# Attention vectors broadcast by DMA, six lead tiles, an early table load and a split last store in a graph-attention and expert-FFN kernel

## The chip, the cores and the metric

The kernel runs on one core of one Trainium2 chip. The metric is device time in microseconds of one execution. A profiled execution gives a trace: its span runs from the first to the last instruction.

## The reference, cut to what matters

```python
# x [30000, 256]; src, dst, edge_type_8 [510000], sorted by dst; 8 relations, 4 heads, head size 64
def _L0_gnn_ref(inputs, conv_weights, attn_l, attn_r, h_bias, edge_src, edge_dst, edge_type):
    feat_all = jnp.einsum('ni,rhid->rnhd', inputs, conv_weights)
    feat_src_e = feat_all[edge_type, edge_src]
    feat_dst_e = feat_all[edge_type, edge_dst]
    el = jnp.sum(feat_src_e * attn_l[edge_type], axis=-1)
    er = jnp.sum(feat_dst_e * attn_r[edge_type], axis=-1)
    e = jax.nn.leaky_relu(el + er, negative_slope=LEAKY_SLOPE)
    ...            # softmax of e over the edges of one destination node gives alpha
    h = jax.ops.segment_sum(alpha[..., None] * feat_src_e, edge_dst, num_segments=N_NODES)
    return h.reshape(N_NODES, OUT_FEAT) + h_bias

x = x + _L0_gnn_ref(_layernorm(x), ...)
x = x + _L0_ffn_ref(_layernorm(x)[None], ...)[0]     # a shared MLP and the best two of four experts
```

For every node, relation and head a vector of 64 features is computed, with two numbers beside it: its product with `attn_l` (the source's share of an edge's score) and with `attn_r` (the destination's share).

## The kernel before

There are two stages, one after the other. A third part of the code is skipped on these inputs: its loops run `again` times, which is zero here.

The **feature stage** goes over the nodes in 235 tiles of 128 (the last has 48 new rows). Each tile is normalised (`norm`: statistics, reciprocal and scaling on VectorE, DVE; the square root on ScalarE, ACT), turned on TensorE, PE, into `xT` (`turn`), and multiplied by all weights in `NG` = 5 groups of columns (`group`, L299: four of 7 heads x 64 = 448 columns, the last of 4 x 64 and 64 more). A float32 matmul goes through PE in two passes, and a group has two matmuls, one for each half of the 256 inputs: four passes. Groups are evicted from PSUM (pool `pf`, six buffers) into `fo`, by ACT or DVE (L301). The 64 columns at the end of `w` give the two attention numbers: L303 puts the source's into `fo`, L307 the destination's into `er`. SyncE's queue, SP, stores `fo` to `feat` in DRAM, 1040 KB a tile (L309). Once for four tiles `dest_pieces` splits `er` into three bfloat16 parts in five DVE operations (L322, L324) and SP stores them to `erp_d`. After the second tile of each four, `residual` lets GpSimd, POOL, add the bias `hb` (L268), and SP stores the sum (`xb_d`) and loads the next four tiles of `x` (`xg`), in that order.

The 64 columns must first be computed: they are the weights' products with `attn_l` and `attn_r`. `attention(s)` does this in 16 slots. Each even slot spreads 512 numbers of an attention vector over all partitions with a matmul of a column of ones (one row deep) by `arow` (L333); two slots use it: a product (L335) and a sum (L337) on DVE. So that PE has work meanwhile, the first `LEAD` = 5 tiles do only their groups 0 to 3, a slot behind each group from slot 0 on; when all slots are done, the lead tiles' group 4 follows for all of them, and from tile 5 on a tile is done whole.

The **edge stage** goes over the edges in 253 blocks. For each, POOL gathers 16 sets of 128 rows of `feat` by index (L751, 4050 gathers in all), DVE computes scores and softmax, PE sums by destination, and the expert MLPs of finished nodes are woven in. Its pools lie where the feature stage's did, so the first gather waits for that stage's last stores, evictions and matmuls. SP loads a block's `rc`, `dr`, `erp` and `xt` two blocks ahead.

In both stages `tc.manual_schedule()` keeps every engine's instructions in the order of the program. DMAs of SP and ACT take eight completion semaphores in turn: a DMA waits until the eighth before it has landed. The stage's first DMAs are issued so: SP the first four tiles of `x`, then the four chunks of `w` for the first half of the inputs, with `attn_l` after the first; ACT the chunks of the second half and `attn_r`. ACT's first `activation` is the square root in `norm(0)` (L129), and the load of its table stands right before it.

Of the kernel before, what the change touches and what calls it, by code (L numbers as in the profile page):

```python
# [10 lines left out]
F32 = mybir.dt.float32  # L11
# [3 lines left out]
AF = mybir.ActivationFunctionType  # L15
# [6 lines left out]
P = 128  # L22
# [3 lines left out]
HD = 64  # L26
HW = HD + 1
# [13 lines left out]
T = 4  # L41
# [7 lines left out]
def kernel(  # L49
# [26 lines left out]
    nc = tc.nc  # L76
    N = x.shape[0]
    E = src.shape[0]
    NT = -(-N // P)
# [25 lines left out]
    eps = const.tile([P, 1], F32, name="eps")  # L105
# [11 lines left out]
    def bcast(dst_ap, src_ap, n):  # L117

        nc.sync.dma_start(dst_ap, bass.AP(tensor=src_ap.tensor, offset=src_ap.offset, ap=[[0, P], [1, n]]))
# [47 lines left out]
    for i in range(NPEN + 1):  # L167
        f = wf.tile([P, H, U if i < NPEN else UL], F32, name=f"penf{i}")
# [44 lines left out]
    with ExitStack() as cx:  # L213
        wp = cx.enter_context(tc.tile_pool(name="wconv", bufs=1))
        xp = cx.enter_context(tc.tile_pool(name="xa", bufs=2))
# [3 lines left out]
        pf = cx.enter_context(tc.tile_pool(name="pf", bufs=6, space=PSUM))  # L219
        RH = R * H  # L220
        NW = RH * HD
        GH = 7
        NG = -(-RH // GH)
        LEAD = 5

        w = wp.tile([P, 2, NW + 2 * RH], F32, name="w")
        arow = wp.tile([1, 2, NW], F32, name="arow")
        ones = wp.tile([1, P], F32, name="ones")
        nc.vector.memset(ones, 1.0)
        featv = feat.rearrange("(n r) f -> n (r f)", r=R)  # L230
        tiles = {}
        quad = {}

        def start(m):
            return min(m * P, N - P)

        def fresh(m):

            return m * P - start(m)

        def per_rows(q, dram_of, sb_of, store):

            if (q + 1) * T * P <= N:
                d, s = dram_of(q * T * P, T * P).rearrange("(j p) f -> p j f", p=P), sb_of(slice(0, P), slice(0, T))
                nc.sync.dma_start(*((d, s) if store else (s, d)))
                return
            for j in range(min(T, NT - q * T)):
                m = q * T + j
                f = fresh(m) if store else 0
                d, s = dram_of(start(m) + f, P - f), sb_of(slice(f, P), j)  # L250
                nc.sync.dma_start(*((d, s) if store else (s, d)))

        def load_x(q):
            if q * T >= NT:
                return
            xg = quad[q] = xp.tile([P, T, D], F32, name="xg")
            if q == 0:
                for j in range(T):
                    nc.sync.dma_start(xg[:, j], x[j * P:(j + 1) * P, :])
            else:  # L260
                per_rows(q, lambda r, n: x[r:r + n, :], lambda p, j: xg[p, j], False)
# [18 lines left out]
        def turn(m, eng):  # L280
# [4 lines left out]
            for k in range(2):  # L285
                nc.tensor.transpose(ptr[:, k, :], t["xn"][:, 0, k * P:(k + 1) * P], ident)  # L286
            t["xT"] = xp.tile([P, 2, P], F32, name="xT", bufs=LEAD + 1)
            eng(t["xT"], ptr)  # L288

        def group(m, g, eng):  # L290

            t = tiles[m]
            if g == 0:
                t["fo"] = xp.tile([P, RH, HW], F32, name="fo", bufs=LEAD + 1)
            h0, h1 = g * GH, min((g + 1) * GH, RH)
            c0, c1 = h0 * HD, h1 * HD if g < NG - 1 else NW + 2 * RH
            ps = pf.tile([P, 512], F32, name="ps")[:, :c1 - c0]
            for k in range(2):
                nc.tensor.matmul(ps, t["xT"][:, k, :], w[:, k, c0:c1], start=k == 0, stop=k == 1)  # L299
            n = (h1 - h0) * HD  # L300
            eng(t["fo"][:, h0:h1, :HD], ps[:, :n].rearrange("p (a d) -> p a d", d=HD))  # L301
            if g == NG - 1:
                nc.vector.tensor_copy(t["fo"][:, :, HD], ps[:, n:n + RH])  # L303
                q, j = divmod(m, T)
                if j == 0:
                    quad[q, "er"] = xp.tile([P, T, RH], F32, name="er")
                nc.vector.tensor_copy(quad[q, "er"][:, j, :], ps[:, n + RH:])  # L307
                f = fresh(m)
                nc.sync.dma_start(featv[start(m) + f:start(m) + P, :],  # L309
                                  t["fo"][f:].rearrange("p a d -> p (a d)"))  # L310
                del tiles[m]
                if j == T - 1 or m == NT - 1:
                    dest_pieces(q, j + 1)

        def dest_pieces(q, n):

            er = quad.pop((q, "er"))
            del quad[q]
            erp = xp.tile([P, T, H, 3, R], BF16, name="erp")
            erv = er.rearrange("p j (r h) -> p j h r", h=H)[:, :n]  # L320
            for k in range(3):
                nc.vector.tensor_copy(erp[:, :n, :, k, :], erv)  # L322
                if k < 2:
                    nc.vector.tensor_sub(erv, erv, erp[:, :n, :, k, :])  # L324
            per_rows(q, lambda r, n: erp_d[r:r + n].rearrange("n h k r -> n (h k r)"),
                     lambda p, j: erp.rearrange("p j h k r -> p j (h k r)")[p, j], True)

        def attention(s):

            i, q, k = s // 8, s // 2 % 4, s % 2  # L330
            if k == 0:
                quad["ab"] = pf.tile([P, 512], F32, name="ps")
                nc.tensor.matmul(quad["ab"], ones, arow[:, i, q * 512:(q + 1) * 512], start=True, stop=True)  # L333
            pr = xp.tile([P, 8, HD], F32, name="pr")
            nc.vector.tensor_mul(pr, quad["ab"].rearrange("p (a d) -> p a d", d=HD),  # L335
                                 w[:, k, q * 512:(q + 1) * 512].rearrange("p (a d) -> p a d", d=HD))
            nc.vector.tensor_reduce(w[:, k, NW + i * RH + q * 8:NW + i * RH + q * 8 + 8], pr, AX.X, ALU.add)  # L337

# [136 lines left out]
            nc.vector.tensor_reduce(bad, two, AX.X, ALU.max)  # L475

        with tc.manual_schedule():
            load_x(0)
            for k in range(2):
                eng = nc.scalar if k else nc.sync  # L480
                for g in range(4):
                    eng.dma_start(w[:, k, g * 512:(g + 1) * 512].rearrange("p (a d) -> p a d", d=HD),
                                  conv_w[2 * g:2 * g + 2, :, k * P:(k + 1) * P, :].rearrange("r h p d -> p (r h) d"))
                    if g == 0:
                        a = attn_r if k else attn_l
                        eng.dma_start(arow[:, k, :], a.rearrange("(o r) h d -> o (r h d)", o=1))
            bcast(hb, h_bias, D)
            norm(0)
            turn(0, nc.scalar.copy)
            norm(1)  # L490

            slot = 0
            lead = min(LEAD, NT)
            for m in range(lead):
                for g in range(NG - 1):
                    group(m, g, nc.scalar.copy)
                    if slot < 16:
                        attention(slot)
                    slot += 1
                    if g == 1 and m + 1 < lead:  # L500
                        turn(m + 1, nc.scalar.copy)
                        norm(m + 2)
            while slot < 16:
                attention(slot)
                slot += 1
            side = [expert_weights(), edge_records()]

            def aside():
                while side:
                    try:  # L510
                        next(side[0])
                        return
                    except StopIteration:
                        side.pop(0)

            for m in range(lead):
                group(m, NG - 1, nc.vector.tensor_copy)
                if m == 1:
                    turn(lead, nc.vector.tensor_copy)
                    norm(lead + 1)  # L520
            for m in range(lead, NT):
                for g in range(NG):
                    group(m, g, nc.scalar.copy if g < NG - 2 else nc.vector.tensor_copy)
                    if g == 1:
                        turn(m + 1, nc.vector.tensor_copy)
                        norm(m + 2)
                    if g == 2:
                        aside()
            while side:
                aside()  # L530

# [634 lines left out]
    with ExitStack() as cx:  # L1166
# [3 lines left out]
        with tc.For_i(0, again * NQ) as q:  # L1170
# [3 lines left out]
            tiles = out[ds(r0, TM), :].rearrange("(j p) f -> j p f", p=M)  # L1174
            g = Experts(xc, ph_p, pc_p, x1, T, lambda t, r: nc.sync.dma_start(tiles[t], r))
# [34 lines left out]
```

## Time and profile before

| what | value |
|---|---|
| median of three runs | 6918.72 us (6917.0 to 6920.45) |
| profiled execution | 6915.86 us |
| its span | 6914.1 us |
| PE busy | 6021.3 us (87%) |
| DVE busy | 5112.5 us (74%) |
| ACT busy | 3445.9 us (50%) |
| POOL busy | 4019.3 us (58%) |
| first matmul of L299 | 10.48 us |
| end of the feature stage on PE | 1742.48 us |
| first gather | 1748.66 us |

Times within the span count from its start. Busy time leaves out the issuing of DMAs, which the timeline shows on an engine's queue (SPq, ACTq, POOLq). Shares over the whole span mix the two stages. A line such as `8.28 0.29 ACT L129 ACTIVATE ...` of the timeline gives start, duration, engine, line and operation; neighbours of one kind are merged (x4), and a bracket tells how long the engine stood idle before and what released it.

### The profile page before, as it was taken

The numbers are of one execution on the slowest core, as the hardware profiler recorded it, in microseconds if no ns is written. First come the engines' busy times: TensorE is split into PE (matmuls) and PEld (weight loads), VectorE is DVE, ScalarE is ACT, GpSimd is POOL, SyncE is SP. The second block draws the span as 40 slices with busy tenths as digits, with TensorE's granted clock in tenths as the row PEclk, the third lists the DMA queues.
The fourth block names the chain that finished last, engine by engine and source line by source line (L and its number), as shares of the span: only waits on it lengthen the run. The fifth ranks groups of instructions, "written<-read, shape, count | busy, mean of one in ns | idle before, by whom it ended". The sixth has DMA issues, their size and how long they took to land. (4 is left out here: it accounts for less than half of the span.)

```text
span 6914.1 us, 95450 instructions
## 1 busy us (share of the span) xinstructions
PE 6021.3 (87%) x25270; PEld 3842.8 (56%) x25271; DVE 5112.5 (74%) x13840; ACT 3445.9 (50%) x9508; POOL 4019.3 (58%) x4174
## 2 busy tenths in 40 slices
PE   9999999999588888888888888888888888888887
PEld 4555555555455555555555555555555555555555
DVE  5555445444688888888888888888888888888885
ACT  2222222222465555555655556555555655555564
POOL 1110000000677777777777777777777777777773
PEclk9999999999799999999999999999999999999999
DMA  5665554554555555555555555555555555555552
GB/s 191 223 227 187 188 187 183 188 186 179 147 150 147 148 154 148 149 150 147 147 149 154 150 147 150 148 148 152 151 150 148 149 147 149 154 150 147 151 147 76
DMA packets 589928, 1097.14 MB, mean 159 GB/s; under 512 B 199445, under 2 KB 428571, under 8 KB 559371
## 3 DMA queue, kind: packets, MB, share of 16 engines
q0 software_dynamic: 194400, 539.40, 27.9%
q1 hardware_dynamic: 390811, 550.45, 24.1%
q8 instruction: 206, 3.38, 0.2%
q14 instruction: 349, 2.86, 0.1%
q10 hardware_dynamic: 4162, 1.06, 0.1%
HBM read 761.91 MB, written 328.62 MB: 158 GB/s over the span
## 5 line engine op out<-in xcount | busy, mean ns | idle before, releaser
L751 POOL DMA_INDIRECT ft<-feat,rc x4050 | 3849.3, 950 | 1288.3 <-issue 512.3
L891 PE MATMUL po<-ft,oh 128*128 128x260 f32 x8100 | 2213.2, 408 | 117.6 <-DVE pen L762 113.8
L891 PEld LDWEIGHTS po<-ft,oh 128*128 128x128 f32 x8100 | 1520.0, 202 | 374.2 <-issue 172.7
L299 PE MATMUL ps<-w,xT 128*128 128x448 f32 (+1 forms) x4700 | 1710.3, 519 | 0.5 <-ACT xT L288 0.5
L884 DVE TENSOR_TENSOR ft<-ft,p 128x768 f32<-128x768 f32 x1518 | 1286.4, 848 | 235.9 <-ACT ft L877 235.9
L828 ACT ACTIVATE oh<-icol,nd 128x128 f32<-128x128 f32 x4050 | 1334.5, 389 | 0.0
L299 PEld LDWEIGHTS ps<-w,xT 128*128 128x128 f32 x4700 | 875.0, 190 | 691.8 <-issue 612.1
L301 ACT COPY fo<-ps 128x448 f32<-128x448 f32 x710 | 378.1, 532 | 1069.9 <-PE ps L299 938.8
L268 POOL TENSOR_TENSOR xb<-xg,hb 128x1024 f32<-128x1024 f32 (+1 forms) x59 | 143.1, 2425 | 1248.3 <-DMA xg<-in_x_dram 1203.1
L829 ACT ACTIVATE oh<-oh 128x384 f32<-128x384 f32 x1518 | 740.1, 488 | 48.1
L805 PEld LDWEIGHTS <-ohT 128*128 128x128 bf16 x4050 | 392.0, 158 | 410.3 <-issue 333.7
L818 DVE TENSOR_REDUCE e<-ere 128x16 f32<-128x384 f32 (+1 forms) x1012 | 561.5, 555 | 34.8
L845 PE MATMUL t<-ident,f 128*4 128x128 f32 x253 | 74.2, 293 | 559.7 <-DVE f L838 519.7
L816 DVE TENSOR_TENSOR ere<-pe,th 128x384 f32<-128x384 f32 (+1 forms) x1012 | 553.9, 547 | 0.0
L628 PE MATMUL ph<-xT,v 128*128 128x512 f32 (+1 forms) x1024 | 513.5, 627 | 1.4 <-ACT h L629 1.0
L876 ACT ACTIVATE p<-e 128x64 f32<-128x64 f32 (+1 forms) x253 | 70.0, 277 | 796.7 <-DVE e L871 795.9
L805 PE MATMUL pe<-erp,ohT 128*128 128x96 bf16 x4050 | 434.4, 232 | 27.5 <-DVE ohT L788 20.4
L301 DVE COPY fo<-ps 128x256 f32<-128x256 f32 x465 | 242.5, 523 | 275.7 <-PE ps L299 275.2
L288 DVE COPY xT<-ptr 128x256 f32<-128x256 f32 x230 | 97.3, 423 | 454.4 <-PE ptr L286 454.4
L845 PEld LDWEIGHTS t<-ident,f 128*4 128x4 f32 x253 | 20.8, 82 | 653.5 <-ACT oh L829 402.9
L833 DVE TENSOR_TENSOR e<-e,ft 128x64 f32<-128x64 f32 (+1 forms) x253 | 69.2, 274 | 411.2 <-DMA ft<-feat,rc 411.1
L788 DVE TENSOR_SCALAR ohT<-dr,rowid 128x2064 bf16<-128x2064 int16 (+1 forms) x253 | 324.3, 1282 | 5.0 <-DMA erp_d<-erp 2.9
(169 smaller groups left out, 6839.9 us busy)
## 6 DMA issues: line engine op xcount, KB each, us to landing
feat<-fo SPq DMA_DIRECT2D x234, 1040.0 KB
dr<-dst SPq DMA_DIRECT2D x252, 516.0 KB
ft<-feat,rc POOLq DMA_INDIRECT x4050
xt<-xb_d SPq DMA_DIRECT2D x253, 128.0 KB
out_dram<-og SPq DMA_DIRECT2D x253, 128.0 KB
xb_d<-xb SPq DMA_DIRECT2D x58, 512.0 KB
xg<-in_x_dram SPq DMA_DIRECT2D x57, 512.0 KB
rc<-rec SPq DMA_DIRECT2D x252, 34.0 KB
```

Of the source, the lines that this page charges most:

```text
L299: nc.tensor.matmul(ps, t["xT"][:, k, :], w[:, k, c0:c1], start=k == 0, stop=k == 1)
L301: eng(t["fo"][:, h0:h1, :HD], ps[:, :n].rearrange("p (a d) -> p a d", d=HD))
L628: nc.tensor.matmul(ps[:, :self.w], lhs, rhs, start=i == 0, stop=i == len(pairs) - 1)
L751: nc.gpsimd.indirect_dma_start(out=s.ft[:, u].rearrange("p h d -> p (h d)"), out_offset=None, in_=feat[:, :], in_offset=bass.IndirectOffse ...
L788: nc.vector.tensor_scalar(ohT[:, :3 * s.dw].rearrange("n (i e) -> n i e", i=3), s.dr[:, :, :s.dw], rowid[:, t:t + 1], None, op0=ALU.is_equal)
L805: nc.tensor.matmul(pe[:, u - u0].rearrange("p f r -> p (f r)"), s.ov[:, u, :], s.erp.rearrange("n h k r -> n (h k r)"), start=True, stop=True)
L816: nc.vector.tensor_mul(ere, s.pe[:, :u1 - u0], s.th[:, u0:u1, None, :].to_broadcast([P, u1 - u0, H * 3, R]))
L818: nc.vector.tensor_reduce(s.e[:, :, u0:u1].rearrange("p h u -> p u h"), ere.rearrange("p u (h k) r -> p u h (k r)", h=H), AX.X, ALU.add)
L828: nc.scalar.activation(s.oh[:, u, :], icol, AF.Abs, bias=s.nd[:, u:u + 1])
L829: nc.scalar.activation(s.oh[:, u0:u1], s.oh[:, u0:u1], AF.Relu, bias=1.0, scale=-1.0)
L884: nc.vector.tensor_mul(fc, fc, pc[:, :, None].to_broadcast([P, (u1 - u0) * H, HD]))
L891: nc.tensor.matmul(s.po.rearrange("n h d -> n (h d)"), s.oh[:, u, :], s.ft[:, u].rearrange("p h d -> p (h d)"), start=u == 0, stop=u == s. ...
```

## The change

- The attention vectors are no longer spread by matmul. Two DMAs on SP write each of them to all 128 partitions of `ab`, 1 MB each, after the weights and before `hb`. `attention` reads `ab`; `arow`, `ones` and the eight matmuls of L333 are gone.
- `LEAD` is 6, and slots start at tile 1 (`slot = -4`): the groups of tiles 0 and 5 have none.
- ACT first takes the square root of `eps` into a scratch tile, which puts the table load at the head of its instructions.
- The chunks of `w` are issued in the order of columns, both halves of the inputs in turn, seven on SP and one (the first of the second half) on ACT.
- The last tile does group 4 first, then 0 to 3, evicted by ACT and DVE in turn (ACT for 4, 0 and 2, DVE for 1 and 3). `dest_pieces` of the last tiles follows group 4. `fo` of that tile is stored in two parts: heads 0 to 20 after group 2, heads 21 to 31 after group 3.
- The store becomes a function of its own; for the other tiles its place in the order is the same.

```diff
@@ -221,12 +221,10 @@
         NW = RH * HD
         GH = 7
         NG = -(-RH // GH)
-        LEAD = 5
+        LEAD = 6
 
         w = wp.tile([P, 2, NW + 2 * RH], F32, name="w")
-        arow = wp.tile([1, 2, NW], F32, name="arow")
-        ones = wp.tile([1, P], F32, name="ones")
-        nc.vector.memset(ones, 1.0)
+        ab = wp.tile([P, 2, NW], F32, name="ab")
         featv = feat.rearrange("(n r) f -> n (r f)", r=R)
         tiles = {}
         quad = {}
@@ -290,7 +288,7 @@
         def group(m, g, eng):
 
             t = tiles[m]
-            if g == 0:
+            if "fo" not in t:
                 t["fo"] = xp.tile([P, RH, HW], F32, name="fo", bufs=LEAD + 1)
             h0, h1 = g * GH, min((g + 1) * GH, RH)
             c0, c1 = h0 * HD, h1 * HD if g < NG - 1 else NW + 2 * RH
@@ -305,12 +303,16 @@
                 if j == 0:
                     quad[q, "er"] = xp.tile([P, T, RH], F32, name="er")
                 nc.vector.tensor_copy(quad[q, "er"][:, j, :], ps[:, n + RH:])
-                f = fresh(m)
-                nc.sync.dma_start(featv[start(m) + f:start(m) + P, :],
-                                  t["fo"][f:].rearrange("p a d -> p (a d)"))
-                del tiles[m]
-                if j == T - 1 or m == NT - 1:
+                if m == NT - 1:
                     dest_pieces(q, j + 1)
+
+        def store(m, h0=0, h1=RH):
+            t, f = tiles[m], fresh(m)
+            nc.sync.dma_start(featv[start(m) + f:start(m) + P, h0 * HW:h1 * HW],
+                              t["fo"][f:, h0:h1].rearrange("p a d -> p (a d)"))
+            q, j = divmod(m, T)
+            if j == T - 1 and m < NT - 1:
+                dest_pieces(q, j + 1)
 
         def dest_pieces(q, n):
 
@@ -328,11 +330,8 @@
         def attention(s):
 
             i, q, k = s // 8, s // 2 % 4, s % 2
-            if k == 0:
-                quad["ab"] = pf.tile([P, 512], F32, name="ps")
-                nc.tensor.matmul(quad["ab"], ones, arow[:, i, q * 512:(q + 1) * 512], start=True, stop=True)
             pr = xp.tile([P, 8, HD], F32, name="pr")
-            nc.vector.tensor_mul(pr, quad["ab"].rearrange("p (a d) -> p a d", d=HD),
+            nc.vector.tensor_mul(pr, ab[:, i, q * 512:(q + 1) * 512].rearrange("p (a d) -> p a d", d=HD),
                                  w[:, k, q * 512:(q + 1) * 512].rearrange("p (a d) -> p a d", d=HD))
             nc.vector.tensor_reduce(w[:, k, NW + i * RH + q * 8:NW + i * RH + q * 8 + 8], pr, AX.X, ALU.add)
 
@@ -475,26 +474,27 @@
             nc.vector.tensor_reduce(bad, two, AX.X, ALU.max)
 
         with tc.manual_schedule():
+            rs = xp.tile([P, 1], F32, name="a_rs")
+            nc.scalar.activation(rs, eps, AF.Sqrt)
             load_x(0)
-            for k in range(2):
-                eng = nc.scalar if k else nc.sync
-                for g in range(4):
+            for g in range(4):
+                for k in range(2):
+                    eng = nc.scalar if (g, k) == (0, 1) else nc.sync
                     eng.dma_start(w[:, k, g * 512:(g + 1) * 512].rearrange("p (a d) -> p a d", d=HD),
                                   conv_w[2 * g:2 * g + 2, :, k * P:(k + 1) * P, :].rearrange("r h p d -> p (r h) d"))
-                    if g == 0:
-                        a = attn_r if k else attn_l
-                        eng.dma_start(arow[:, k, :], a.rearrange("(o r) h d -> o (r h d)", o=1))
+            for i, a in enumerate((attn_l, attn_r)):
+                bcast(ab[:, i, :], a, NW)
             bcast(hb, h_bias, D)
             norm(0)
             turn(0, nc.scalar.copy)
             norm(1)
 
-            slot = 0
+            slot = -4
             lead = min(LEAD, NT)
             for m in range(lead):
                 for g in range(NG - 1):
                     group(m, g, nc.scalar.copy)
-                    if slot < 16:
+                    if 0 <= slot < 16:
                         attention(slot)
                     slot += 1
                     if g == 1 and m + 1 < lead:
@@ -515,10 +515,11 @@
 
             for m in range(lead):
                 group(m, NG - 1, nc.vector.tensor_copy)
+                store(m)
                 if m == 1:
                     turn(lead, nc.vector.tensor_copy)
                     norm(lead + 1)
-            for m in range(lead, NT):
+            for m in range(lead, NT - 1):
                 for g in range(NG):
                     group(m, g, nc.scalar.copy if g < NG - 2 else nc.vector.tensor_copy)
                     if g == 1:
@@ -526,6 +527,13 @@
                         norm(m + 2)
                     if g == 2:
                         aside()
+                store(m)
+
+            for g in (NG - 1, *range(NG - 1)):
+                group(NT - 1, g, nc.vector.tensor_copy if g % 2 else nc.scalar.copy)
+                if g == NG - 3:
+                    store(NT - 1, 0, (NG - 2) * GH)
+            store(NT - 1, (NG - 2) * GH)
             while side:
                 aside()
 
```

## The prediction

> **What bounds the kernel now.** I read the page's slices first, since a share over the whole span mixes two stages. Each digit is the busy share of 1/40 of the span, 173 us.
>
> ```profile
> PE   9999999999588888888888888888888888888887
> DVE  5555445444688888888888888888888888888885
> POOL 1110000000677777777777777777777777777773
> ```
>
> For ten slices only PE is full: the feature stage. Then POOL takes over, and the page's costliest group says how:
>
> ```profile
> L751 POOL DMA_INDIRECT ft<-feat,rc x4050 | 3849.3, 950 | 1288.3 <-issue 512.3
> ```
>
> 4050 gathers of 0.95 us with 0.30 us before each. In the timeline of POOL the first starts at 1748.66 and the last at 6830.56: 5081.9 us over 4049 steps, 1.255 us a step, and the waits view finds no wait of POOL before a gather over 0.3 us after the first. So the edge stage is a rigid chain: the span ends 6914.1 - 1748.66 = 5165.4 us after the first gather, whatever went before. What the change is worth is how much earlier that gather starts.
>
> In the feature stage the waits view of PE (0 to 1745 us) has two lines: PE starts late, then never waits.
>
> ```profile
> PE ptr L286 <- DVE a_xn L133: 9.4, 1, 9.4
> PE ps L299 <- ACT xT L288: 0.5, 1, 0.5
> ```
>
> The timeline (start, duration, engine, what) shows what it starts behind, what the first matmuls cost, and the lead:
>
> ```profile
> 4.16 0.18 DVE L127 BATCH_NORM_AGGREGATE a_mv<-a_st 128x2 f32<-128x6 f32 x1
> 4.80 2.16 ACTq L482 DMA_DIRECT2D w<-_L_gnn_conv_weights_dram  x3
> 6.98 1.28 ACT L129 ACT_TABLE_LOAD   x1 [6.85 <-issue]
> 8.28 0.29 ACT L129 ACTIVATE a_rs<-a_mv,eps 128x1 f32<-128x1 f32 x1
> 10.48 3.36 PE L299 MATMUL ps<-w,xT 128*128 128x448 f32 x4 [0.46 <-ACT xT L288]
> 13.77 2.07 PE L333 MATMUL ps<-arow,ones 1*128 1x512 f32 x2
> 18.98 1.67 PE L299 MATMUL ps<-w,xT 128*128 128x448 f32 x4
> 47.82 9.94 PE L299 MATMUL ps<-w,xT 128*128 128x448 f32 x28
> ```
>
> The statistics of tile 0 are ready at 4.34, but ACT issues weight loads and then loads its table until 8.26. Four passes (one group) take 3 us at 10.48 and 1.5 us later: PE is at half speed until 18.7. The last fence is the end of the stage:
>
> ```profile
> 1731.14 11.34 PE L299 MATMUL ps<-w,xT 128*128 128x448 f32 x32
> 1743.17 0.32 DVE L322 CAST erp<-er 128x96 bf16<-128x96 f32 x1
> 1744.61 0.32 DVE L322 CAST erp<-er 128x96 bf16<-128x96 f32 x1
> 1744.95 1.38 SPq L251 DMA_DIRECT2D erp_d<-erp  x3
> 1747.56 0.35 SPq L744 DMA_DIRECT2D erp<-erp_d  x1
> 1748.66 1.14 POOL L751 DMA_INDIRECT ft<-feat,rc  x1 [54.68 <-issue]
> ```
>
> PE ends at 1742.48, and the gather starts 6.18 us later, behind five `erp` operations on DVE, three stores of `erp_d` and their landing, which SP's wait dates to about 1747.45.
>
> **What the skill says.** "ScalarE: Activation LUTs" (What ACT_TABLE_LOAD costs) gives 1283 ns for the load; the trace agrees (1.28). "TensorE: Matmul & The Clock Gate" (Part 1) has PE at half rate until about 3.4 us of sustained work, counted in free-running windows. The trace agrees on the factor, not the time: from 10.48 to 18.7 PE is busy and slow for 8 us, with L333's one-row matmuls in between. "DMA: Bandwidth & Descriptors" (Rules for kernel authors) says that DMAs of several queues share the same 16 engines; so moving weight loads from ACT's queue to SP's moves issue time, not bandwidth.
>
> **The change, part by part.**
>
> *Table first.* `Sqrt` of `eps` and its load go to the head of ACT: 0.84 + 1.28 + 0.3 = 2.4. ACT then issues one weight load (0.48) and is free at 3.0, before 4.34. From there by the same durations: sqrt 0.3, reciprocal 0.2, normalise 0.45, two transposes 0.7, copy 0.45: first matmul at 6.5. It also needs both weight chunks of columns 0 to 511. The traffic line of the first 20 us shows the first 1.05 MB moved by about 6; with ACT's chunk issued 1.6 us later I take 6.7. Against 10.48: 3.8 us earlier. Bounds: 6.5 and 8.0.
>
> *Weights in order of columns.* SP now issues seven of the eight chunks, three more at about 0.45 us each. The traffic line shows about 217 GB/s from 8 to 13.5, so the last chunk lands at about 14, as before. Group 3 of tile 0 needs it for its second half, at 14.6 below: hidden, with 0.6 us to spare.
>
> *L333 gone.* Eight matmuls of one row leave PE. The first took 2.0 (13.77 to 15.77, slow). From 18.98 to 47.82 PE did 13 groups (19.5), three transposes (0.66) and the other seven: 28.84 - 20.16 = 8.7, 1.24 each, more than the 1.05 between starts.
>
> *Slow phase.* I assume that the skill's window holds once L333 is gone: full speed between 10.1 and 13.4; middle 11.7. Then group 0 of tile 0 runs 6.7 to 9.7, group 1 to 12.2, transposes 0.2, group 2 to 13.9, group 3 to 15.4. Before, two such groups end at 18.98 + 3.0 = 21.98 without the L333 between. Gain 6.6, and with the seven 8.7: **15.3 us**. If PE stays slow for 8.3 us again, group 3 ends at 17.05 (1.65 less); if it warms at once, the last chunk holds it to 14.9 (0.5 more).
>
> *`ab` by DMA.* 2.1 MB more in the queue, ahead of `hb`. At the rate of the lead's feature stores (about 420 GB/s between 57 and 75) that is 5.0 us; at that of the weights 9.7. No row shows this broadcast; 5.0 is taken, as its rows are 8 KB like those of `fo`. `hb` landed at 14.6 (POOL's wait), so now at 19.5; behind it on POOL stands only `xb`, but the second quad of `x` is queued on SP behind the store of `xb`, and landed 7.4 us after `hb` (22.0): now 26.9. DVE waits for it in the norm of tile 4, with ten attention slots queued behind. A slot is 1.37 (two from 47.93 to 50.67), a norm 1.6: DVE finishes at 26.9 + 1.7 + 13.7 + 3.2 = 45.5.
>
> *Six lead tiles.* Tiles 1 to 4 carry the slots, tile 5 none. PE: 15.4, four tiles of 6.22, tile 5 in 6.0: first last-group at 46.3. It needs all slots: 0.8 us to spare. DVE's 7.1 us a tile against PE's 6.22 costs nothing only by that cover; later `ab` costs PE one for one. The sixth `fo`, 0.6 us more on DVE and one store more in the burst fall where PE ran on before.
>
> *Last tile.* Its group 4 goes first, so the `erp` chain and its stores finish under groups 1 to 3. Behind PE's end T stay: DVE's 448-column eviction (0.66), SP's issue (from T + 0.7), the landing of 137 KB in place of 390. The old store was on the wire from about 0.8 us after its issue for 2.6 us; a third of the bytes 0.9, receipt 0.4: T + 2.8. The first part (262 KB), issued at about T - 0.9, is out of the way by T + 1.7. From landing to gather 1.2 as before: T + 4.0 to 4.1 against T + 6.18. **Gain 2.1**, bounds 1.2 and 2.8 (if the landing is all fixed time; if none of it is).
>
> *Sum.* 15.3 + 2.1 = 17.4. The profiled execution took 6915.86 (span 6914.1 and 1.8 around), so it would take 6898.5; the median of the runs is 2.9 above it, and the same saving puts the median at **6901.3**.
>
> **Rivals.**
>
> 1. *DVE becomes the bound of the lead* (12%). If `ab` moves at the weights' rate, `x` lands at 31.6, the slots end at 50.2, PE stands 3.9 us before the last groups: saving 13.5, 6905.2, just within no change. For: the cover is 0.8 us. Against: 8 KB rows.
> 2. *The gather step grows* (6%). In the built program's order every DMA of the edge stage takes a completion slot one further on, so SP's loads wait for other transfers; if gathers then wait for late `rc`, a step costs more. It decides from 17.4 / 4049 = 4.3 ns a step, and 8 ns more (32 us) gives 6933, slower. Against: `rc` is loaded a whole block (20 us) ahead, and no gather waited more than 0.3.
> 3. *The table load is no gain* (5%): the first chunk lands only at 10, late behind ACT's. Then 3.3 goes back: 14.1, 6904.6. Against: 1.05 MB stood on the wire by 6.
>
> **How the numbers follow.** The likeliest case has 77%; its own range is a saving of 14 to 19.5 (slow phase -1.65/+0.5, tail -0.9/+0.7, the runs' spread of 3.4). A measurement tells some 0.2%, 13.8 us, from no change. Down to rival 1 the range is 6897 to 6908. Faster: most of the likeliest and of rival 3, 0.79; within 0.2%: rival 1 and the rest, 0.15; slower: rival 2, 0.06.
>
> **What would show it.** Right: ACT_TABLE_LOAD at about 0.8; first L299 at 6.5 to 7; no L333 on PE; 1.5 us groups from 10 to 13.4; PE at last-groups at about 46; first gather 4.1 us after PE's end and at about 1731; gather step still 1.255. Wrong: PE waiting for DVE `w` or `xn` in the lead (rival 1), POOL waits over 0.3 (rival 2), a first matmul at 8 or later (rival 3), or PE slow past 15.

## The result and the profile after

The changed kernel takes 6902.91 us (median of 16 runs, 6900.34 to 6908.02) against 6917.81 (median of 16 runs of the kernel before beside it, 6913.39 to 6920.45): 14.9 us less, ratio 0.998, 95% interval 0.9972 to 0.9988. Predicted was 6901.3. Its profiled execution took 6906.35 (span 6904.7), 3.4 above its own median, where that of the kernel before (6915.86) stood 1.95 below its median. In the last set of runs below (e9 to e12) the edge stage was slower in every kernel, the one before too (its median there is 8641.16), so those four are compared only with one another and with that median.

The slices and the costliest group look as they did; the waits of PE up to 1730 us, shown last, do not:

```profile
PE   9999999999588888888888888888888888888887
DVE  5555444454688888888888888888888888888885
POOL 1110000000777777777777777777777777777773
```

```profile
L759 POOL DMA_INDIRECT ft<-feat,rc x4050 | 3851.7, 951 | 1285.8 <-issue 472.5
```

```profile
PE ptr L284 <- DVE a_xn L133: 5.0, 1, 5.0
PE ps L297 <- DMA w<-_L_gnn_conv_weights_dram: 1.6, 1, 1.6
```

PE starts behind 5.0 us of DVE in place of 9.4, and a new wait stands behind it: the matmul is ready and its weights are not there. The timeline (start, duration, engine, what; a bracket is idle time and its releaser) shows both ends of the feature stage:

```profile
0.84 1.28 ACT L478 ACT_TABLE_LOAD   x1 [0.70 <-PEq L1206]
3.90 0.29 ACT L129 ACTIVATE a_rs<-a_mv,eps 128x1 f32<-128x1 f32 x1 [1.56 <-DVE a_mv L127]
5.68 0.37 ACT L286 COPY xT<-ptr 128x256 f32<-128x256 f32 x1 [1.49 <-PE ptr L284]
7.24 5.84 PE L297 MATMUL ps<-w,xT 128*128 128x448 f32 x8 [1.60 <-DMA w<-_L_gnn_conv_weights_dram]
13.13 6.18 PE L297 MATMUL ps<-w,xT 128*128 128x448 f32 x16
...
38.39 11.34 PE L297 MATMUL ps<-w,xT 128*128 128x448 f32 x32
46.89 0.69 DVE L336 TENSOR_REDUCE w<-pr 128x8 f32<-128x512 f32 x1
...
1724.81 1.28 SPq L249 DMA_DIRECT2D erp_d<-erp  x3
1727.30 1.91 SPq L311 DMA_DIRECT2D feat<-fo  x2
1728.25 0.62 DVE L299 COPY fo<-ps 128x448 f32<-128x448 f32 x1 [2.38 <-PE ps L297]
1729.55 0.37 SPq L752 DMA_DIRECT2D erp<-erp_d  x1
1732.57 1.14 POOL L759 DMA_INDIRECT ft<-feat,rc  x1 [52.31 <-DMA xt<-xb_d]
```

The table load is at 0.84. The eight passes of groups 0 and 1 run from 7.24, nearly all at half speed; the clock record has full speed from 12.47 (from 18.59 before). No L333 is left. The last slot's sum on DVE ends at 47.57 just as PE reaches the first last-group (its first matmul, inside the line of 38.39, is at 47.41). At the other end the stores of `erp_d` are issued at 1724.81, ahead of PE's end at 1728.21, and the gather follows that end by 4.36 us where it was 6.18.

So PE ends 14.27 us earlier (1742.48 to 1728.21) and the first gather comes 16.09 earlier (1748.66 to 1732.57). The profiled span fell by only 9.4, because from the first gather on this execution took 5172.1 us and that of the kernel before 5165.4. The medians put most of that difference down to the execution: they differ by 14.9, so of the 16.1 some 1.2 us are missing, not 6.7. The next sections ask what each edit gave, and where the missing time is.

### The profile page after: what moved, and what is told of

It is laid out like the page before. It is cut to its first block, busy times and chain, and to the rows that moved or that the text cites. A ratio compares the mean times of both kernels' runs of the same rounds, so it can differ in the third digit from the quotient of the medians.

```text
span 6904.7 us, 95411 instructions
## 1 busy us (share of the span) xinstructions
PE 6024.9 (87%) x25254; PEld 3851.5 (56%) x25255; DVE 5113.0 (74%) x13837; ACT 3445.3 (50%) x9511; POOL 4018.5 (58%) x4174
## 5 line engine op out<-in xcount | busy, mean ns | idle before, releaser
L759 POOL DMA_INDIRECT ft<-feat,rc x4050 | 3851.7, 951 | 1285.8 <-issue 472.5
L297 PE MATMUL ps<-w,xT 128*128 128x448 f32 (+1 forms) x4700 | 1707.7, 518 | 1.6 <-DMA w<-_L_gnn_conv_weights_dram 1.6
L297 PEld LDWEIGHTS ps<-w,xT 128*128 128x128 f32 x4700 | 875.8, 190 | 689.2 <-issue 611.0
L299 ACT COPY fo<-ps 128x448 f32<-128x448 f32 (+1 forms) x711 | 377.5, 532 | 1054.1 <-PE ps L297 915.6
L299 DVE COPY fo<-ps 128x448 f32<-128x448 f32 (+1 forms) x464 | 242.3, 523 | 266.6 <-PE ps L297 263.9
```

What stands on the lines that cost most here:

```text
L759: nc.gpsimd.indirect_dma_start(out=s.ft[:, u].rearrange("p h d -> p (h d)"), out_offset=None, in_=feat[:, :], in_offset=bass.IndirectOffse ...
```

## The experiments

All start from the changed kernel; a run without a median was executed once, under the profiler. Here is where each stood. The last column is what lies between PE's end and the first gather; times are in us from the start of the span, and "full clock" is from the trace's clock record.

| kernel | first L297 | full clock from | last slot ends on DVE | first last-group | PE ends | first gather | after PE's end |
|---|---|---|---|---|---|---|---|
| before | 10.48 | 18.59 | 50.66 | 55.44 | 1742.48 | 1748.66 | 6.18 |
| after | 7.24 | 12.47 | 47.57 | 47.41 | 1728.21 | 1732.57 | 4.36 |
| e1 no early square root | 7.48 | 13.04 | 47.55 | 47.50 | 1728.30 | 1732.45 | 4.15 |
| e2 weights on ACT | 9.07 | 11.87 | 46.84 | 47.73 | 1728.53 | 1732.91 | 4.38 |
| e3 spread by matmul | 7.38 | 10.62 | 51.45 | 56.23 | 1737.03 | 1741.38 | 4.35 |
| e4 five lead tiles | 7.15 | 10.35 | 45.34 | 44.16 | 1733.21 | 1737.55 | 4.34 |
| e5 old tail | 7.64 | 12.84 | 48.67 | 48.51 | 1729.32 | 1735.55 | 6.24 |
| e6 warmed PE | 7.15 | 5.32 | 47.21 | 47.05 | 1727.85 | 1731.94 | 4.09 |
| e7 warmed, early x | 6.60 | 6.09 | 49.13 | 50.03 | 1730.83 | 1735.21 | 4.38 |
| e8 no sums on POOL | 7.17 | 13.01 | 45.68 | 47.33 | 1728.13 | 1732.50 | 4.37 |

In some rows the first last-group starts before the last slot ends. Its first matmul needs only the columns of the first half of the inputs, and the slot before the last completes those: in e4 it starts at 44.16, behind the sum that ends at 44.02, and the matmul for the second half only at 45.39, behind the last sum's end at 45.34.

How far do two traces of one kernel differ? e12 is the changed kernel again, and its first gather is at 1731.80 against 1732.57; e11 is e5 again, with 1735.14 against 1735.55. So a difference of less than about 0.8 us at the gather between two single traces is not told from none.

**The start, e1 and e2.** e1 drops the early square root; e2 gives the second half of the weights back to ACT.

```diff
 # e1
-            rs = xp.tile([P, 1], F32, name="a_rs")
-            nc.scalar.activation(rs, eps, AF.Sqrt)
 # e2
-                    eng = nc.scalar if (g, k) == (0, 1) else nc.sync
+                    eng = nc.scalar if k else nc.sync
```

> Only the square root of eps at the head of ACT is left out. Theory (ACT was late before because three weight loads that wait for completion slots stood ahead of its table load; with one load there the table comes early by itself): table load over by about 3, first matmul at 7.2 as in the changed kernel, first gather at 1732.6 within 0.3. Rival (the early square root is what brings the start): table load after the statistics of tile 0, first matmul at 8.5 or later, first gather 1.3 or more later. From the first gather to the end: 5165 to 5173 if that part only varies from run to run.

> The changed kernel, but ACT again issues all four chunks of the second half of the weights; the early square root stays. Theory (the issues on ACT cost the start): ACT is free at about 6.4, first matmul at about 8.6 (1.4 later), first gather at about 1733.8 (1.2 later). Rival (the chunks' landing sets the start, whoever issues): first matmul at 7.2, first gather at 1732.6.

In e1 the table load comes by itself behind ACT's one remaining DMA issue, 0.5 us later, and nothing at the gather is worse (1732.45):

```profile
0.84 0.47 ACTq L481 DMA_DIRECT2D w<-_L_gnn_conv_weights_dram  x1
1.35 1.28 ACT L129 ACT_TABLE_LOAD   x1 [1.21 <-PEq L1204]
```

In e2 ACT issues its third and fourth chunk until 6.82, with tile 0's square root right behind them at 6.86 (3.90 in the changed kernel). The timeline:

```profile
3.46 3.36 ACTq L483 DMA_DIRECT2D w<-_L_gnn_conv_weights_dram  x2
```

The first matmul is 1.83 later, the gather 0.34, where 1.2 was expected. Two things eat the rest. Full clock came 0.6 earlier in this execution, so less of the work ran at half speed; tile 0's group 2 begins at 13.77 against 13.13. And half of that 0.64 is gone by the first last-group (47.73 against 47.41), since in the changed kernel PE's weight load waits 0.8 us for DVE before tile 5. So it is the weights leaving ACT that makes the early start of PE; what that start is worth at the gather, 0.34 here, is not told from none. The early square root, with the weights gone from ACT, is not seen in the time.

**The matmuls, e3.** `arow`, `ones` and the spreading matmuls are back, all else as changed.

```diff
 # e3, cut: the tiles arow and ones are back too, and the product reads quad["ab"]
+            if k == 0:
+                quad["ab"] = pf.tile([P, 512], F32, name="ps")
+                nc.tensor.matmul(quad["ab"], ones, arow[:, i, q * 512:(q + 1) * 512], start=True, stop=True)
-                bcast(ab[:, i, :], a, NW)
+                nc.sync.dma_start(arow[:, i, :], a.rearrange("(o r) h d -> o (r h d)", o=1))
```

> The changed kernel with the attention vectors spread by the eight one-row matmuls again, in tiles 1 to 4; arow is loaded where ab was. Theory (each costs PE 1.24 us, and PE is the bound of the lead): first gather at 1742.4 (9.8 later), median 9.8 above the changed kernel, so about 6912.7 or 5 below the kernel before. Rival 1 (only 1.05 each, by their starts): first gather at 1740.9. Rival 2 (the gain of 15 us came from elsewhere): first gather under 1736.

PE ends 8.82 later and the gather is 8.81 later. Median 6913.71 (13 runs) against 6917.51 for the kernel before beside it, ratio 0.9994, interval 0.9985 to 1.0002: without the broadcast the change is not told from none. The group of the first 60 us on PE:

```profile
L337 PE MATMUL ps<-arow,ones 1*128 1x512 f32 x16 | 9.0, 640 | 0.0
```

Busy time 9.0 is not the whole price. From tile 0's group 2 (12.29 here, 13.13 in the changed kernel) to the first last-group PE took 43.94 against 34.28: 9.66 for eight, 1.21 each, where they start 1.05 apart from what follows. This is the largest single part of the saving.

**The lead, e4.** `LEAD` back to 5, slots still from tile 1.

> The changed kernel with five lead tiles. Theory (DVE ends the slots at 47.6 whatever PE does, and in the changed kernel PE comes to the first last-group at 47.4, just then): PE comes at 41.4 and stands until 47.6, 6 us or more, since it may lose its full speed while it stands; first gather 6 to 9 later, at 1738.6 to 1741.6. Rival (the slots are done long before): PE does not stand, first gather at 1732.6.

The gather is 5.0 later, less than the 6 to 9 expected: DVE ends the slots at 45.34 and not at 47.57, since no norm of tile 5 stands between them. PE runs out of work and then pays once more; the waits of PE in the first 52 us, and two stretches with the busy times of PE, its loader, DVE, ACT and POOL, the granted clock, and the DMA share and rate:

```profile
PE ps L297 <- DVE w L336: 4.2, 1, 4.2
```

```profile
41.20:44.40 3.20, 0.24 (x1) 0.27 (x2) 3.13 (x6) 0.00 (x0) 0.00 (x0) 1.00 0.00 0
44.40:47.90 3.50, 3.37 (x7) 1.75 (x7) 1.52 (x5) 0.00 (x0) 0.00 (x0) 0.51 0.02 5
```

PE stands 4.2 us for the slots, and the next 3.4 us run at half clock, which by estimate costs another 1.7; about 1.1 of the sum is hidden by a full clock that came 2.1 earlier at the start. The sixth tile is needed to cover the slots, as the diff has it.

**The tail, e5.** The last tile in its old order and with one store, after group 4.

> The changed kernel with the last tile in the old order and one store of its features. Theory (the split tail was worth 1.8): the first gather comes 6.2 after PE's end, at 1734.4. Rival (the landing of the last store is a fixed time and the order alone matters little): 4.5 or less after PE's end.

```profile
1730.01 0.32 DVE L322 CAST erp<-er 128x96 bf16<-128x96 f32 x1
1731.78 1.39 SPq L249 DMA_DIRECT2D erp_d<-erp  x3
1735.55 1.14 POOL L752 DMA_INDIRECT ft<-feat,rc  x1 [54.19 <-issue]
```

In the timeline the casts and the stores of `erp_d` fall behind PE's end (1729.32) again, and the gather follows it by 6.24 against 4.36. Over all traces, e9 to e12 included, the split tail gives 4.09 to 4.38 (ten traces) and the old one 6.18 to 6.40 (four). Yet this execution took 6903.21: from its first gather to the end it took only 5166.0. That question is taken up with e9.

**What bounds the lead, e6 to e8.** e6 runs matmuls on zeros before the first tile, so that the clock is up early. e7 adds to e6 an early start of the first weights and loads the second quad of `x` ahead of the store of `xb`. e8 stores `x` in place of `xb` for the first three quads, which takes POOL's sums out of the lead.

```diff
 # e6
+            ...              # warm and its tile of zeros (memset on DVE)
+            warm(512)        # 128 x 512 zeros times 128 x 128 zeros into a bank of pf
+            warm(512)
             turn(0, nc.scalar.copy)
+            warm(448)
 # e7, in norm: load_x(q + 1) before residual(q); in load_x(0): w chunk (0, 0) behind x tile 0
-                residual(q)
                 load_x(q + 1)
+                residual(q)
 # e8, in residual
+            if q < 3:
+                per_rows(q, lambda r, n: xb_d[r:r + n, :], lambda p, j: xg[p, j], True)
+                return
```

> The changed kernel with three matmuls of zeros on PE (512, 512 and 448 columns; two before the first transposes, one after) whose results nobody reads. Theory on the clock[...]: the first group of tile 0 takes 1.5 to 2 instead of 3, group 3 ends at about 15 instead of 16.1. Theory on the bound (DVE's slots, not PE, set the first last-group): that group still starts at 47.5 and the first gather stays at 1732.6 within 0.3. Rival (PE is the bound): first gather 1.1 earlier.

> The kernel of the zero matmuls, and two orders on SP changed: the first weight chunk goes out right behind the first tile of x, and the next four tiles of x are loaded before the sum with the bias is stored, not behind it. Theory: first matmul at 6.2 to 6.6, the second quad of x lands at about 21 instead of 27.8, DVE ends the slots at about 45.4, the first last-group starts at about 46, first gather at 1731.1 (1.4 earlier); the median moves by as little and can't be told from the changed kernel's. Rival (DVE's end is set by the slots and not by x): first last-group at 47.5, first gather at 1732.6.

> The changed kernel without POOL's addition of the bias for the first twelve tiles: x itself is stored there, so that the output of their nodes lacks the bias. Theory (a TENSOR_SCALAR of DVE that overlaps a POOL operation ends 0.15 after it): the three normalisations of the lead that took 1.50, 1.23 and 1.28 take 0.41, DVE ends the slots at about 43 to 44.7, PE doesn't wait there and the first gather moves by 0.2 at most (1732.4). Rival (the broadcast or other DMA traffic slows DVE): they still take over 1.

e6 has full clock from 5.32, 7.2 us earlier, and PE ends 0.36 earlier; the gather's 0.63 is not told from none. In its timeline tile 0's later groups wait for their weights (0.19 and 0.28), and then tile 5 waits for DVE:

```profile
37.76 0.44 PE L284 MATMUL ptr<-ident,a_xn 128*128 128x128 f32 x2 [0.90 <-DVE a_xn L133]
```

What PE gained at the start it stands off before the last tile of the lead: DVE's slots and norms have become a limit equal to PE.

e8 shows what makes DVE late. In the timeline of the changed kernel a normalisation that meets one of POOL's sums takes three times its time:

```profile
27.81 2.36 POOL L266 TENSOR_TENSOR xb<-xg,hb 128x1024 f32<-128x1024 f32 x1 [5.33 <-DMA xg<-in_x_dram]
29.09 1.23 DVE L133 TENSOR_SCALAR a_xn<-xg,a_mv,a_rs 128x256 f32<-128x256 f32 x1
35.54 2.36 POOL L266 TENSOR_TENSOR xb<-xg,hb 128x1024 f32<-128x1024 f32 x1 [5.38 <-issue]
36.78 1.28 DVE L133 TENSOR_SCALAR a_xn<-xg,a_mv,a_rs 128x256 f32<-128x256 f32 x1
```

With POOL idle, in e8:

```profile
28.88 0.41 DVE L133 TENSOR_SCALAR a_xn<-xg,a_mv,a_rs 128x256 f32<-128x256 f32 x1
35.75 0.41 DVE L133 TENSOR_SCALAR a_xn<-xg,a_mv,a_rs 128x256 f32<-128x256 f32 x1
```

DVE ends its slots 1.89 earlier, and the gather moves by 0.07: PE waits for DVE no longer, and comes to the first last-group 0.08 earlier. So two limits lie on each other, which is why neither e6 nor e8 gains alone. Both edits in one kernel were not run.

e7 was to gain by an earlier `x`; it lost 2.6 at the gather against the changed kernel. Its timeline:

```profile
19.56 4.71 POOL L268 TENSOR_TENSOR xb<-xg,hb 128x1024 f32<-128x1024 f32 x2 [15.29 <-DMA hb<-in_L_gnn_h_bias_dram]
21.99 2.83 DVE L336 TENSOR_TENSOR pr<-ab,w 128x512 f32<-128x512 f32 x1
27.54 2.35 POOL L268 TENSOR_TENSOR xb<-xg,hb 128x1024 f32<-128x1024 f32 x1 [3.27 <-DMA xg<-in_x_dram]
28.10 2.33 DVE L336 TENSOR_TENSOR pr<-ab,w 128x512 f32<-128x512 f32 x1
32.80 0.44 PE L286 MATMUL ptr<-ident,a_xn 128*128 128x128 f32 x2 [2.28 <-DVE a_xn L133]
```

`x` came early, so POOL ran its sums two in a row and the third sooner, against DVE's slots. Two products of `ab` and `w` took 2.83 and 2.33 in place of 0.68, and one normalisation 1.57: 5.0 us of DVE. PE stood 2.28 for tile 4, and the clock record shows half speed from 33.40 to 36.81 after it. That it is the second operand in SBUF that lets a product be held is seen in e3, where the same product reads its vector from PSUM. There one started inside a sum of POOL and took its usual time:

```profile
22.41 2.36 POOL L268 TENSOR_TENSOR xb<-xg,hb 128x1024 f32<-128x1024 f32 x1 [5.28 <-DMA xg<-in_x_dram]
22.52 0.69 DVE L339 TENSOR_TENSOR pr<-ps,w 128x512 f32<-128x512 f32 x1 [0.22 <-PE ps L337]
```

Timed, e7 is 6911.92 (21 runs) against 6923.77 on its chip, ratio 0.9983, interval 0.9976 to 0.9989. So it keeps most of the change's saving and adds none.

**The missing microseconds, e9 to e12.** In every split-tail trace up to here the time from first gather to end is 5171.9 to 5177.0, in the two with the old tail 5165.4 and 5166.0. Part of the difference lies behind the start of the last gather, where the same work of PE takes longer at a lower granted clock; the kernel before and the changed one (columns as in e4):

```profile
6830.56:6914.10 83.54, 59.68 (x230) 37.93 (x230) 26.16 (x86) 20.84 (x44) 1.42 (x4) 0.85 0.06 18
6816.88:6904.70 87.82, 63.91 (x230) 40.65 (x230) 26.16 (x86) 20.92 (x44) 1.51 (x4) 0.78 0.05 17
```

With the old tail this stretch is 83.5 and 83.2 us (before, e5), at a clock of 0.85; in the eight traces with the split tail it is 86.4 to 88.7, at 0.78 to 0.81. The rest lies in the steps from the first gather to the last, 5081.9 and 5082.8 us against 5084.3 to 5088.9. The last four runs ask for the cause. The split tail has one DMA more on SP, so in the edge stage each DMA takes the next completion slot. Three theories: the slots (S), the split tail itself (T), or chance (V). The four kernels cross tail and slots; the number of DMAs is changed away from the tail, in the load of the last three tiles of `x`.

```diff
 # e9: split tail, one DMA fewer (slots in the edge stage as before)
+                if q == (NT - 1) // T:
+                    nc.sync.dma_start(xg[:, 0:2], x[q * T * P:(q * T + 2) * P, :].rearrange("(j p) d -> p j d", p=P))
+                    nc.sync.dma_start(xg[:, 2], x[N - P:N, :])
+                    return
 # e10: old tail, one DMA more (slots shifted): the same place, tile 0 of the three in two halves
 # e11: e5 again; e12: the changed kernel again
```

> The changed kernel, split tail and all, with one DMA fewer on SP near the end of the feature stage: the last three tiles of x are loaded in two DMAs in place of three. That brings the eight completion slots in the edge stage back to where they stand in the kernel before. Theory S (the shifted slots make the edge stage longer): first gather at 1732.5 as in the changed kernel, from there to the end 5166 us and not 5172 to 5177, and the median 16 to 20 us below the kernel before, which would beat both kernels. Theory T (the split tail itself does it): 5172 to 5177 and the same median as the changed kernel. Theory V (one execution differs from another by this much, and the two short stages were chance): no order between the four kernels of this set but the gather's, 14 to 16 us below before.

> The changed kernel with the tail of the kernel before (last tile in the order 0 to 4, one store), and one DMA more on SP near the end of the feature stage: the last three tiles of x are loaded in four DMAs in place of three. The slots in the edge stage then stand as in the changed kernel. First gather at 1735 in all theories. Theory S (shifted slots): 5172 to 5177 us from there to the end, and 7 to 12 us below the kernel before. Theory T (split tail): 5166, and 13 to 14 below. Theory V (chance): any length, 12 to 14 below.

> The old tail alone once more (the same kernel as e5), now timed. First gather at 1735, 2 to 3 us later than in the changed kernel. Theories S and T (shifted slots, or the split tail): 5166 us from the first gather to the end again, and a median no higher than the changed kernel's, 13 to 15 below the kernel before. Theory V (chance): a length anywhere from 5166 to 5177, and a median about 2 above the changed kernel's.

> The changed kernel once more, so that the other three of this set have it on their chip. First gather at 1732.5, 16.1 us before that of the kernel before. Theories S and T: 5172 to 5177 us from there to the end, median 15 below the kernel before. Theory V (chance): a length anywhere from 5166 to 5177, median 14 to 16 below.

| kernel | tail, slots | first gather | from there to the end, profiled execution | median (runs) | below before | ratio, 95% interval |
|---|---|---|---|---|---|---|
| e9 | split, as before | 1731.99 | 6886.8 | 8629.96 (21) | 11.2 | 0.9981 (0.9973 to 0.9989) |
| e12 | split, shifted | 1731.80 | 6899.8 | 8633.31 (13) | 7.9 | 0.9987 (0.9976 to 0.9999) |
| e10 | old, shifted | 1734.07 | 6897.7 | 8636.89 (13) | 4.3 | 0.9996 (0.9987 to 1.0004) |
| e11 | old, as before | 1735.14 | 6885.5 | 8640.32 (13) | 0.8 | 0.9999 (0.9991 to 1.0007) |

The ratio is an estimate from all runs and not the quotient of the two medians, from which it differs by up to 0.0006 here.

The feature stage came out as on the other occasions. The edge stage did not; of e12, the first by the page, the second by the groups of PE:

```profile
L759 POOL DMA_INDIRECT ft<-feat,rc x4050 | 3844.5, 949 | 2991.7 <-PE pe L813 1081.1
```

```profile
L636 PE MATMUL ph<-xT,w 128*128 128x512 f32 x504 | 369.8, 863 | 1195.5 <-issue 1026.9 <-ACT xT L582 168.6
```

and the same group of PE in the changed kernel's first profile:

```profile
L636 PE MATMUL ph<-xT,w 128*128 128x512 f32 x504 | 237.1, 593 | 0.0
```

A gather took 0.95 us as ever, but POOL stood 2991.7 us before gathers in place of 1285.8, most of all for PE, and PE stood 1195.5 us before the first layer of the experts. That layer reads `xT`, which ACT copies at L582, and it is ACT that stood; of e12 and of the changed kernel's first profile, by the groups of ACT:

```profile
L582 ACT COPY xT<-ph 128x512 f32<-128x512 f32 (+1 forms) x128 | 73.4, 574 | 1518.1 <-remote 1390.0 <-issue 101.8 <-PE ph L580 21.6
L582 ACT COPY xT<-ph 128x512 f32<-128x512 f32 (+1 forms) x128 | 74.2, 580 | 339.4 <-PE ph L580 336.7
```

In e12 65 of these stands, up to 25.2 us long, end on an event that the profile can give to no instruction ("remote"). The other three kernels of the set have the same 1512.5 to 1527.8 us before this copy. What ACT waited for is open. A slower PE explains little: its busy time grew by 325 us (6024.9 to 6349.6), the time from first gather to end by 1728. So this set has no rigid chain behind the gather, and a medians' difference in it is not in one-to-one relation with the gather's.

The single profiles, read alone, would speak for S: 6886 with the slots as before, 6898 to 6900 with them shifted. The medians do not follow: with the split tail the slots as before are 3.3 us better, with the old tail 3.4 us worse, and neither is told from none where the runs of one kernel spread over 31 to 57 us. e11's profiled execution was the fastest of its 13, 18 us below their median. T gets no support: both split tails lie below both old ones, by 3.6 us at the least, where T has the old tail no worse; only the split tails' intervals exclude no change. V's order (the gather's, in which e9 and e12 are level) holds, its amounts (12 to 16 us below before) do not. In short, neither S nor T is supported; that chance explains all of the first sets is not shown either. There the runs of one kernel spread over 7.7 us (changed) and 7.1 (before), as much as the two groups of traces differ by. What remains to be explained in medians is 1.2 us in the changed kernel (16.1 at the gather, 14.9 timed), 3.5 in e3 (7.3 and 3.8) and 1.6 in e7 (13.45 and 11.85). Each lies inside the interval of its own medians (for the changed kernel 8.3 to 19.4 us of saving), so no loss is shown. But all three have the same sign, and the split tail and the shifted slots in common; some 1 to 3 us of real loss in the edge stage may be there, and its cause stays open.

## Why the prediction was right

The median came out 1.6 us above the forecast and inside the range, through the mechanism that was named: an earlier start of PE, no one-row matmuls and a shorter tail bring the first gather forward. The closeness is in part luck. The saving fell 2.5 us short of the 17.4 forecast, 1.3 of it before the gather and 1.2 behind it, and 0.9 of that was given back because the kernel before, at 6917.81 over 16 runs, was faster than the 6918.72 over three from which the forecast started. By its steps:

| step | predicted | measured |
|---|---|---|
| table load | 0.8 | 0.84 |
| first L297 | 6.7 | 7.24 |
| full clock | 11.7 | 12.47 |
| group 3 of tile 0 ends | 15.4, gain 6.6 | 16.13, gain 5.85 |
| seven L333 at 1.24 | 8.7 | 8.5 (eight at 1.21 in e3, seven of them) |
| hb landed / second quad of x landed | 19.5 / 26.9 | 20.1 / 27.8 |
| DVE ends the slots | 45.5 | 47.57 |
| first last-group on PE | 46.3, 0.8 spare | 47.41, nothing spare |
| gather after PE's end | 4.0 to 4.1, gain 2.1 | 4.36, gain 1.82 |
| first gather | about 1731 | 1732.57 |
| gather step | 1.255 | 5084.3 / 4049 = 1.256 |

**The start** was mis-sized by 0.54. The chain through ACT and DVE was ready at 6.05 (`xT` copied), earlier than the 6.5 worked out; it was the weights that came late. The step from "the first 1.05 MB moved by about 6", with 0.7 added, is the one that fell short. In the changed kernel, too, 1.09 MB had moved by 6 (182 GB/s over the first 6 us), but the two chunks were complete only at 7.0 to 7.6 in the traces in which PE waited for them: a sum of traffic does not tell which transfers are complete.

**The full clock** was argued from the Trainium skill's "TensorE: Matmul & The Clock Gate" (Part 1), against the trace of before, and it came inside the range worked out, 5.2 us after the first L297 in place of 8.1. Over the kernels without zero matmuls it came between 2.8 us (e2) and 5.8 us (e8) after the first L297, so a figure such as 11.7 has some 1.5 us of play on either side, half of which reaches the time. That the one-row matmuls made it 8.1 before is not shown: no run has them back among the groups of tile 0.

**L333** was sized right, and by the right reading: the price of a one-row matmul is what PE's timeline loses around it, 1.2, not its busy time.

**DVE's end** is the step that failed, by 2.1 us. 0.9 of it is the later `x`, and 1.7 are two norms behind it that met POOL's sums (1.23 and 1.28 in place of 0.41); ten slots at 1.32 in place of 1.37 gave 0.5 back. The step is "a norm 1.6", which takes its duration from rows in which POOL was idle. The Trainium skill's "SBUF — State Buffer" (SBUF: two separate sides) says that DVE and GpSimd share a port pair that one instruction holds to its end, for DVE operations in a two-port mode, or with two SBUF inputs against a GpSimd operation that reads SBUF. That L133 runs in a two-port mode no run here shows. The traces agree that it is held: it ends 0.15 us after POOL's sum ends (22.62 and 22.47, 30.32 and 30.17, 38.06 and 37.90), and with the sums gone (e8) it is 0.41 again. The move from `quad["ab"]` in PSUM to `ab` in SBUF also makes the product an operation with two SBUF inputs; e7 shows such products held up, and e3 one with a PSUM input that is not. None of this was in the prediction. It cost little because PE came to the first last-group 1.1 late itself, 0.7 of it from the start, so that the forecast's 0.8 to spare was used up but hardly exceeded: the only wait for DVE in PE's lead behind the first tile was that of a weight load, 0.8 us, before tile 5. DVE as the bound of the lead, rival 1, was thus nearer than its 12% said, and by another cause than the DMA rate that it named: `hb`, behind the broadcast, landed at 20.1 where 19.5 was worked out.

**The tail** was right within 0.3 us: the store's landing and what follows took 4.09 to 4.38 where 4.0 to 4.1 was said.

**The edge stage** was taken as rigid, at 5165.4. In the profiled execution it was 6.7 longer, in medians 1.2 (with the gather's time of one trace for all). Rival 2, a longer gather step with waits over 0.3 us, did not come: no gather of the first profile waited longer. But the prediction's test, one execution against one, could not have told 1 us from 7, and it took the stretch behind the last gather as fixed, where the traces have 83.2 to 88.7 us.

## What to carry to other kernels

Price an operation from rows in which its neighbours were as they will be: a VectorE duration taken where GpSimd was idle is too low where both will run, and moving an operand from PSUM to SBUF can put an operation into that contention. When several edits bring two engines' ends together, as PE and DVE here at 47.4 and 47.6, further edits to either alone give almost nothing. And don't build a cause on the lengths of two profiled executions when the runs of one kernel spread by the same amount: cross the suspects, and read medians.

## What was not expected of the hardware

- VectorE's normalisation (0.41 us) stretched to between 0.73 (e2) and 1.98 us (e3) in the leads of twelve traces, each time ending 0.15 us after the end of the GpSimd sum that it met; the product of two SBUF operands stretched from 0.68 to 2.83 and 2.33 (e7), and with one operand in PSUM it did not (0.69 in e3).
- PE's clock fell to half for 3.41 us after a stand of 2.28 us in e7, and after one of 4.2 us in e4, in the midst of dense work. So a wait of 2 us in a matmul stage cost up to 1.7 us more than itself.
- One-row matmuls between the first groups went with 8.1 us of half clock before, and 2.8 to 5.8 without them there; matmuls on zeros from 1.59 gave full clock at 5.32 (e6).
- The same two programs took from first gather to end 5172.1 us (changed) and 5166.0 (old tail) in the first sets and 6899.8 and 6885.5 in the last, with ACT standing over 1500 us before one group of copies in place of 339.4 (changed). The traces do not show for what.
